# When the last node tiles choose their experts, and what fills the queues meanwhile

## The chip, the core and the metric

The kernel runs on one core of a Trainium2 chip. The core has five engines, each with its own in-order queue of instructions: PE (matrix products and transposes), DVE (element-wise work), ACT (activation functions, copies), POOL, which here issues the indirect transfers (gathers and scatters by a list of row numbers), and SP, which issues plain transfers. They wait for one another by semaphores. The metric is the device time of one execution in microseconds (us); a kernel is judged by the median over several runs.

## The reference

The program takes 6250 nodes with 256 features and 106250 edges (50000 random pairs in both directions, and a loop at each node). It applies four layers, each after a layer norm and with a residual: a two-step graph network (GIN), an attention over learned slices, a graph convolution (GCN), and a mixture of eight experts, of which each node uses two. Only the last two matter here:

```python
h = x @ W
msgs = h[src] * norm[:, None]
out = segment_sum(msgs, dst) + b
y = (out - running_mean) * rsqrt(running_var + BN_EPS) * gamma + beta
x = x + relu(y)

gate_logits = layernorm(x) @ Wg + bg + bias
topk_vals, topk_idx = top_k(gate_logits, 2)
topk_w = softmax(topk_vals)
h = relu(einsum('td,edh->teh', x_flat, W1) + b1)     # 256 -> 512, each expert
y = einsum('teh,ehd->ted', h, W2) + b2               # 512 -> 256
x = x + sum over the two chosen experts of topk_w * y
```

## The kernel before, in words

Nodes are worked on in 49 tiles of 128 rows (the last has 106). The end of the program joins the graph convolution and the experts in one stream; everything that the change touches is in it.

**Messages.** The edges, sorted by destination, are cut into 782 chunks of 128. For a chunk, POOL gathers the 128 source rows (`msg<-T`, by `gather`, L168) into a ring of 14 buffers, DVE builds a 0/1 matrix that says which row goes to which node (`hot`, L256), and PE multiplies the two in three products (L189, the table being kept in three bf16 pieces). A tile has 16 chunks, the last one 10. POOL issues up to 14 chunks ahead (`fetch_next` in `Sums.__call__`); `sums.n` counts the chunks issued and `others.n` is 782. When the chunks of half a tile are done, `add3` adds them into the tile's sum `s` (L1470, L1473).

**Slots.** While a tile's chunks are multiplied, `Sums.__call__` calls `between` seven times, evenly spread. Each call is a slot: `between_products(t, k)` with k from 0 to 6 puts other work there. Since PE, DVE, ACT and SP run their instructions in the order in which this code writes them, what is put in a slot stands in each of those queues between the tile's matmuls. `now[0]` counts slots, 7 to a tile.

**Choice.** `choice(i, ts, sent_at)` is a generator with seven steps for two tiles together: transpose the sums; multiply by the folded weights, add the residual (L1507 to L1512) and take the norm's statistics; finish the norm (L371 to L375); transpose; compute the gate's logits and the two best experts (L1528 to L1562); nothing; and places in the experts' lists (L1567 to L1577) with the shares (L1548 to L1551). One step is done per slot. It ends by putting the tiles into `to_send`.

**Send.** `send` scatters the tiles' rows into the DRAM table XD at their places, two scatters a tile on POOL (L1586). Then `advance` (L1610 to L1649), 24 small DVE instructions, works out which expert and first row each block of 128 rows will have. It is called where the count of issued messages reaches `sent_at`, or in the drain.

**Blocks.** A block is 128 rows of one expert: fetched by SP (`xd`, L1672, after two register loads, L1668 and L1669), transposed (L1693), multiplied by W1 (`ph`, L1699), transposed (L1705), activated on ACT (L1708), multiplied by W2 (`py`, L1713), given its bias on DVE (`yd`, L1714) and stored back in XD by SP (L1715). Two blocks overlap: a cycle of two pieces does the first half of one and the second half of the block before it. One piece goes into each slot (`next(block_pieces)`). SP keeps up to four blocks fetched ahead; yd has two buffers.

**Parts.** Tiles 0 to 39 are the first part, with its own table and 87 blocks; tiles 40 to 48 are the second, with 25. How many blocks of the second part may be started depends on the tiles sent: 1 after four tiles, 5 after six, 7 after seven, 9 after eight, all 25 after nine.

**Combine.** When all of a part's blocks are written into the program, its tiles enter `to_combine`. `combine` gathers a tile's two result rows per node (`g`, two gathers on POOL, L168, from a ring of eight buffers) and leaves an `end` to be run some slots later: two additions on DVE (L1752), and an output store on SP (L1494) once more than `keep` results are waiting.

**Drain.** After the last tile a loop goes on until nothing is left of choices, sends and blocks. Each step advances every choice, sends what is to be sent, does one piece of a block, and combines one tile. What is left of the combining follows in a second loop.

Before the change tiles 46 and 47 are chosen together during tile 48, tile 48 alone in the drain; pieces of blocks stop after the third slot of tile 48; nothing of the first part is combined before the drain.

Of the kernel before, what the change touches and what calls it, by code (L numbers as in the profile page):

```python
# [21 lines left out]
def gin_transolver_gcn_moe(ctx: ExitStack, tc: tile.TileContext, a: dict, out: bass.AP):  # L22
# [17 lines left out]
    NT = -(-N // P)  # L40
# [17 lines left out]
    def rows_of(t):  # L58
        return min(P, N - t * P)
# [11 lines left out]
    class Chunks:  # L71
# [5 lines left out]
        def start(self, k):  # L77

            return 0 if k <= 0 else self.n if k > 2 * NT - 2 else min(self.n, self.per * (2 * k + 1) // 4)

    all_edges, others = Chunks(E), Chunks(E - N)
# [85 lines left out]
    def gather(msg, table, ix):  # L167
        return nc.gpsimd.indirect_dma_start(out=msg, out_offset=None, in_=table,  # L168
                                            in_offset=bass.IndirectOffsetOnAxis(ap=ix, axis=0))
# [5 lines left out]
    def in_order(ins, gathers=True):  # L175
        for other in behind if gathers else behind[:1]:
            tc.add_manual_dep(ins.ins, other.name,
                              mybir.DependencyInfo(mybir.DependencyClass.NoSync,
                                                   mybir.DependencyReason.SCHED_ONLY),
                              reason="GpSimd's order")  # L180
        if gathers:
            behind.clear()
        behind.append(ins.ins)
# [274 lines left out]
    parts, Bs = [], []  # L458
    for upto, size in ((0.81, P), (1.0, P)):
        ts = [t for t in range(sum(map(len, parts)), NT) if (t + 0.5) / NT <= upto]  # L460
# [676 lines left out]
    if True:  # L1137
# [287 lines left out]
        sums = Sums(others, T3, None, 0, None, None, None)  # L1425
# [51 lines left out]
    sent = [[] for _ in parts]  # L1477
# [3 lines left out]
    TG, AHEAD = 2, 4  # L1481
# [3 lines left out]
    def load_ahead(t):  # L1485

        for u in range(t, min(t + 5, NT)):
            if u not in s3s:
                s3s[u] = w.tile([P, D], F32, name="s3", bufs=7)
                nc.sync.dma_start(s3s[u], S3[u])  # L1490

    def flush(keep):
        while len(outs) > keep:
            nc.sync.dma_start(*outs.pop(0))  # L1494
# [86 lines left out]
    def send(i, ts, xn):  # L1581

        for j, t in enumerate(ts):
            r = rows_of(t)
            for c in range(2):
                ins = nc.gpsimd.indirect_dma_start(  # L1586
                    out=XD[i], out_offset=bass.IndirectOffsetOnAxis(ap=place[:r, t, c:c + 1], axis=0),
                    in_=xn[:r, j, :], in_offset=None)
                in_order(ins, False)
                for other in sent[i] + taken[i] + stored[i]:  # L1590
                    tc.declare_no_dep(ins.ins, other, reason="no two rows go to one place")
                sent[i].append(ins.ins)
        final = ts[-1] == parts[i][-1]
        which = advance(i, final)
        rows = 2 * P * (ts[-1] + 1 - parts[i][0])
        n = n_blocks[i] if final else max(0, -((NE * (Bs[i] - 1) - rows) // Bs[i]))
        fresh.extend((i, which, no, len(sent[i])) for no in range(n_due[i], n))
        n_due[i] = n
# [57 lines left out]
    def load_experts(t):  # L1656

        for e in range(max(0, 2 * t), min(2 * t + 2, NE)):
            n = KD * HID
            nc.sync.dma_start(wx[:, e, :n].rearrange("p (k f) -> p k f", f=HID),  # L1660
                              a["L1_ffn_W1"][e].rearrange("(k p) f -> p k f", p=P))
            nc.sync.dma_start(wx[:, e, n:].rearrange("p (k f) -> p k f", f=D),
                              a["L1_ffn_W2"][e].rearrange("(k p) f -> p k f", p=P))
# [64 lines left out]
    due, fresh, ready, left = [], [], [], {i: n for i, n in enumerate(n_blocks)}  # L1728
    to_send, to_combine, ends = [], [], []
    n_due = [0 for _ in parts]  # L1730
    SLOTS = 7
    now = [0]

    def fetch_more():
        while len(ready) < AHEAD and due:
            b = due.pop(0)
            ready.append((b[0], fetched(*b)))

    def combine(when):

        i, t = to_combine.pop(0)
        r = rows_of(t)
        o = xr[:r, t, :]
        gs = []
        for c in range(2):
            g = w.tile([P, D], F32, name="g", bufs=8)
            in_order(gather(g[:r], XD[i], place[:r, t, c:c + 1]))
            gs.append(g[:r])

        def end():  # L1750
            for c in range(2):
                nc.vector.scalar_tensor_tensor(o, gs[c], share_of[:r, t, c:c + 1], o, op0=OP.mult, op1=OP.add)  # L1752
            flush(4)
            outs.append((out[t * P:t * P + r, :], o))
        ends.append((when, end))

# [8 lines left out]
    def blocks():  # L1765

        while True:
            pending[:] = block_of(*ready.pop(0)) if ready else None, pending[0]
            now_, last = pending
            for it in pending:  # L1770
                if it is not None:
                    next(it)
            if now_ is not None or last is not None:
                yield
            if now_ is not None:
                next(now_)
            if last is not None:
                next(last, None)
                pending[1] = None
            yield  # L1780

    block_pieces = blocks()

    def between_products(t, k):
        if k in (1, 4) and t + 1 < NT:
            of = 2 * t + 2 + k // 4
            if of <= 2 * NT - 2:
                sums.hot(of, start(of))
        if t >= EARLY // 2 and chains and next(chains[0], chains) is chains:
            chains.pop(0)  # L1790

        if t < NT - 1 or k < SLOTS // 2:
            next(block_pieces)
        run_ends()

    def run_ends():
        now[0] += 1
        while ends and ends[0][0] <= now[0]:
            ends.pop(0)[1]()

    def new_blocks():
        due.extend(fresh)
        fresh.clear()
        fetch_more()

    sums.beside = beside
    for i, ts_ in enumerate(parts):
        for q in range(0, len(ts_), TG):
            ts = ts_[q:q + TG]
            for t in ts:  # L1810
                load_ahead(t)
                load_experts(t - 1)
                s = s3s[t]

                nc.vector.scalar_tensor_tensor(s, xr[:, t, :], ln3[:, 0, t:t + 1], s, op0=OP.mult, op1=OP.add)
                k = iter(range(SLOTS))

                def between():
                    n = next(k, None)
                    if n is not None:  # L1820
                        between_products(t, n)

                now[0] = t * SLOTS
                sums(t, between, SLOTS)
                for n in k:
                    between_products(t, n)
                new_blocks()
            chains.append(choice(i, ts, min(others.n, start(2 * ts[-1] + 2) + 3 * others.per // 2)))
    while chains or to_send or due or ready or pending != [None, None]:
        for it in list(chains):  # L1830
            if next(it, chains) is chains:
                chains.remove(it)
        if to_send:
            send(*to_send.pop(0)[1:])
            new_blocks()
        next(block_pieces)
        if to_combine:
            combine(now[0] + 3)
        run_ends()
    while to_combine or ends:  # L1840
        if to_combine:
# [27 lines left out]
```

## Time and profile before

| what | value |
|---|---|
| median of 9 runs | 3551.62 us (3540.61 to 3554.55) |
| the profiled execution, its own time | 3544.95 us |
| its span, first to last instruction | 3542.5 us |
| PE busy in the span | 2803.3 us (79%) |
| POOL busy in the span | 2522.8 us (71%) |
| DVE busy in the span | 1647.7 us (47%) |
| ACT busy in the span | 866.6 us (24%) |
| mean granted PE clock | 0.919 |

A row of a timeline reads: start, duration (us), engine, line, operation, written tile, read tiles, shapes, number; in brackets the idle time of the engine before it and what ended that. A row of the chain that ended last has start, duration and the work or transfer. A row of the table of stretches has the stretch, its length, then for PE, weight loads, DVE, ACT and POOL the busy time and the number of instructions, then the granted PE clock (1.00 is full), the DMA engines' share and GB/s. "issue" means that the engine waited for nothing that the profile shows. Of the 190 us after tile 46 the table of stretches gives:

| stretch, us | PE busy | DVE busy | POOL busy | PE clock |
|---|---|---|---|---|
| 3300 to 3360 | 58.50 | 31.09 | 45.37 | 1.00 |
| 3360 to 3412 | 39.95 | 27.57 | 29.65 | 0.80 |
| 3412 to 3455 | 41.13 | 19.92 | 32.63 | 1.00 |
| 3455 to 3500 | 37.98 | 19.94 | 33.64 | 1.00 |
| 3500 to 3542.5 | 3.82 | 10.48 | 18.45 | 0.59 |

### The profile page before, as it was taken

The page shows a single profiled execution, that of the slowest core. Times are in us where ns is not written, and L with a number is a line of the kernel's source. Part 1 is how long each engine was busy: PE and PEld are TensorE (multiplying, and loading weights), DVE is VectorE, ACT ScalarE, POOL GpSimd, SP SyncE. Part 2 cuts the span into 40 slices and gives each one's busy share as a digit, 9 for nine tenths or more (in the row PEclk, how much of TensorE's full clock was granted, in tenths as well). Part 3 has the DMA queues.
Part 4 walks back from the last instruction along what each step waited for, and adds up shares of the span by engine and source line. Part 5 has one row for each costly group of instructions (what it writes and reads, how often), then busy time and mean ns, then how long its engine had stood idle before and what let it go on. Part 6 is the DMA issues. An engine that isn't in the chain of part 4 may idle for free.

```text
span 3542.5 us, 42536 instructions
## 1 busy us (share of the span) xinstructions
PE 2803.3 (79%) x12790; PEld 1701.6 (48%) x12854; DVE 1647.7 (47%) x4180; ACT 866.6 (24%) x1737; POOL 2522.8 (71%) x2618
## 2 busy tenths in 40 slices
PE   2667777777789699999999997956777777778984
PEld 1333344333346254454455444844555555556653
DVE  5465772232222254455554454754444444444453
ACT  4111111111113022212222122511222223323442
POOL 3777777777776677777777771377777777777765
PEclk7699999999999899999999998976888888889988
DMA  8667888888886899898889883785666666667656
GB/s 273 189 211 245 250 249 264 261 266 265 254 256 222 326 324 302 303 312 303 303 306 307 306 298 134 247 285 173 192 193 192 193 191 190 190 190 209 202 175 178
DMA packets 356553, 861.62 MB, mean 243 GB/s; under 512 B 60132, under 2 KB 158702, under 8 KB 356322
## 3 DMA queue, kind: packets, MB, share of 16 engines
q0 software_dynamic: 174688, 611.60, 55.9%
q1 hardware_dynamic: 175122, 237.62, 19.4%
q10 hardware_dynamic: 6512, 9.63, 0.8%
q8 instruction: 106, 1.74, 0.2%
q14 instruction: 125, 1.02, 0.1%
HBM read 691.35 MB, written 167.27 MB: 242 GB/s over the span
## 4 chain that ended last, share of the span: by engine, by line
PE 31%; DMA 22%; issue 5%; POOL 5%; DVE 2%; ACT 2%; POOLq 0%; ACTq 0%; DVEq 0%; SPq 0%
DMA msg<-T,srcT 14%; PE pa L189 8%; PE pa L283 5%; PE ph L1699 4%; PE py L1713 4%; POOL msg L168 3%; DMA XD<-xn,place 3%; DMA msg<-T2f,srcT 2%; DMA g<-XD,place 2%; PE ptok L1299 2%; PE pl L1274 2%; PE p L1250 1%; PE pt L417 1%; PE pn L1507 1%; PE po L1439 1%
## 5 line engine op out<-in xcount | busy, mean ns | idle before, releaser
L168 POOL DMA_INDIRECT msg<-T,srcT x2017 | 1944.7, 964 | 650.5 <-issue 265.2
L189 PE MATMUL pa<-msg,hot 128*128 128x256 bf16 (+2 forms) x5988 | 1127.9, 314 | 482.3 <-DMA msg<-T,srcT 462.4
L189 PEld LDWEIGHTS <-hot 128*128 128x128 bf16 x6177 | 622.2, 102 | 1148.2 <-issue 840.8
L256 DVE SCALAR_TENSOR_TENSOR hot<-dstT,node 128x1024 bf16<-128x1024 f32 (+2 forms) x255 | 310.4, 1218 | 30.4 <-PE pa L189 17.8
L168 POOL DMA_INDIRECT msg<-T2f,srcT x256 | 243.4, 951 | 78.0 <-issue 37.5
L283 PE MATMUL pa<-msg,hotf 128*128 128x512 f32 x512 | 244.6, 599 | 10.3 <-DMA msg<-T2f,srcT 9.8
L672 DVE TENSOR_TENSOR dinv<-dinv,pa 128x1 f32<-128x1 f32 x145 | 22.2, 153 | 453.7 <-PE pa L189 417.0
L1699 PE MATMUL ph<-wx,xdT 128*128 x448 | 214.1, 600 | 8.1 <-DVE yd L1714 4.7
L1713 PE MATMUL py<-wx,hT 128*128 x896 | 213.6, 381 | 0.7 <-ACT hT L1708 0.7
L1024 PE MATMUL p<-h1T,W1b 128*128 128x512 f32 (+2 forms) x480 | 206.8, 529 | 0.1
L1033 PE MATMUL p<-W2a,h2T 128*128 128x512 f32 x392 | 205.6, 613 | 0.0
L1713 PEld LDWEIGHTS py<-wx,hT 128*128 128x128 f32 x896 | 168.7, 190 | 65.0 <-issue 41.2
L301 DVE SCALAR_TENSOR_TENSOR s<-s,own,pa 128x512 f32<-128x512 f32 x97 | 71.9, 741 | 183.2 <-PE pa L189 115.1
L1708 ACT ACTIVATE hT<-pt,wb 128x128 f32<-128x128 f32 x448 | 127.7, 368 | 44.6 <-PE pt L1705 42.4
L283 PEld LDWEIGHTS pa<-msg,hotf 128*128 128x128 f32 x512 | 90.9, 190 | 94.0 <-issue 53.7
L168 POOL DMA_INDIRECT wx<-T,srcT x42 | 44.9, 1070 | 126.1 <-DVE ln L391 104.0
L1714 DVE TENSOR_TENSOR yd<-py,wb 128x256 f32<-128x256 f32 x112 | 47.2, 422 | 180.6 <-PE py L1713 179.0
L1586 POOL DMA_INDIRECT XD<-xn,place x98 | 97.7, 997 | 43.4 <-issue 29.2
L168 POOL DMA_INDIRECT msg<-T1f,srcT x80 | 86.5, 1081 | 56.4 <-DVE b1b L164 32.3
L1473 DVE TENSOR_TENSOR s<-s,pa 64x256 f32<-64x256 f32 x96 | 40.2, 419 | 185.4 <-PE pa L189 183.9
L168 POOL DMA_INDIRECT g<-XD,place x98 | 96.3, 982 | 39.4 <-issue 14.9
L1701 ACT ACTIVATE h<-ph 128x512 f32<-128x512 f32 x112 | 66.9, 597 | 213.1 <-PE ph L1699 213.1
(404 smaller groups left out, 3786.8 us busy)
## 6 DMA issues: line engine op xcount, KB each, us to landing
XD<-zeros SPq DMA_DIRECT2D x204, 256.0 KB
msg<-T,srcT POOLq DMA_INDIRECT x2017, 4.2
T<-tp SPq DMA_DIRECT2D x49, 384.0 KB
wb<-WB SPq DMA_DIRECT2D x112, 130.0 KB
xd<-XD SPq DMA_DIRECT2D x112, 128.0 KB
XD<-yd SPq DMA_DIRECT2D x112, 128.0 KB
T2f<-tf SPq DMA_DIRECT2D x49, 256.0 KB
s<-T2f SPq DMA_DIRECT2D x23, 512.0 KB
```

Of the source, the lines that this page charges most:

```text
L168: return nc.gpsimd.indirect_dma_start(out=msg, out_offset=None, in_=table, in_offset=bass.IndirectOffsetOnAxis(ap=ix, axis=0))
L189: ins = nc.tensor.matmul(pa[:, :n], hot, msg[:, s * F:s * F + n], start=(start and s == 2), stop=(stop and s == 1))
L256: nc.vector.scalar_tensor_tensor(hot[:, :n, :], self.edges.dst[:, c0:c0 + n, None].to_broadcast([P, n, P]), float(k * HALF), node2[:, k % ...
L283: self.last = nc.tensor.matmul(pa[:, :n], hot, msg[:, :n], start=ends[0], stop=ends[1])
L301: return nc.vector.scalar_tensor_tensor(at, at, times[rows], pa[rows, :F], op0=OP.mult, op1=OP.add)
L1024: nc.tensor.matmul(p[:, :T], W1b[:, k, m * P:(m + 1) * P], h1T[:, k, :T], start=(k == 0), stop=(k == KH - 1))
L1033: nc.tensor.matmul(p, h2T[:, k, j * P:(j + 1) * P], W2a[:, k, :], start=(k == 0), stop=(k == KH - 1))
L1274: nc.tensor.matmul(p, xnT[:, k, j * P:(j + 1) * P], Weff[:, k, :], start=(k == 0), stop=(k == KD - 1))
L1586: ins = nc.gpsimd.indirect_dma_start(out=XD[i], out_offset=bass.IndirectOffsetOnAxis(ap=place[:r, t, c:c + 1], axis=0), in_=xn[:r, j, :], ...
L1699: nc.tensor.matmul(p[:, :HID], xdT[:, k, :], W1[:, k, :], start=(k == 0), stop=(k == KD - 1))
L1708: nc.scalar.activation(hT[:, m, :], pt[:, m * P:(m + 1) * P], AF.Relu, bias=b1[:, m:m + 1])
L1713: nc.tensor.matmul(p[:, :D], hT[:, m, :], W2[:, m, :], start=(m == 0), stop=(m == KH - 1))
```

## The change

Four edits. In the last part, pairs are formed for the first six tiles only, so that tiles 46, 47 and 48 are each chosen by themselves; the choice of 46 runs in the slots of tile 47, that of 47 in the slots of tile 48. Pieces of blocks go into all seven slots of the last tile. A new function `behind_last` does, in a slot, what the drain does in a step: send what is to be sent, and combine a tile; it is called in every slot in which all 782 message chunks have been issued, and in the drain. Until all rows of the last part have been scattered it combines in odd slots only. And the output stores wait behind one further result, not four, once the last block is written.

```diff
         def end():
             for c in range(2):
                 nc.vector.scalar_tensor_tensor(o, gs[c], share_of[:r, t, c:c + 1], o, op0=OP.mult, op1=OP.add)
-            flush(4)
+            flush(4 if left[len(parts) - 1] else 1)
             outs.append((out[t * P:t * P + r, :], o))
...
-        if t < NT - 1 or k < SLOTS // 2:
-            next(block_pieces)
+        next(block_pieces)
+        if sums.n == others.n:
+            behind_last()
         run_ends()
+
+    def behind_last():
+
+        if to_send:
+            send(*to_send.pop(0)[1:])
+            new_blocks()
+        if to_combine and (len(sent[-1]) == 2 * len(parts[-1]) or now[0] % 2):
+            combine(now[0] + 3)
...
     for i, ts_ in enumerate(parts):
-        for q in range(0, len(ts_), TG):
-            ts = ts_[q:q + TG]
+        n_pairs = (len(ts_) - 2) // TG if i == len(parts) - 1 else len(ts_)
+        for ts in [ts_[q:q + TG] for q in range(0, len(ts_), TG)][:n_pairs] + [[t] for t in ts_[n_pairs * TG:]]:
...
         for it in list(chains):
             if next(it, chains) is chains:
                 chains.remove(it)
-        if to_send:
-            send(*to_send.pop(0)[1:])
-            new_blocks()
+        behind_last()
         next(block_pieces)
-        if to_combine:
-            combine(now[0] + 3)
         run_ends()
```

## The prediction

> **What bounds the kernel now.** I read the page first (span, section 2), then the chain of work that ended last from 3405 us on, then the timelines of POOL, DVE and PE around the last tiles, then the table of stretches. The change reaches only what comes after tile 46, the last 190 of 3542.5 us, so only that is worked out. The chain, backwards:
>
> ```profile
> 3485.06 3.77 DMA g<-XD,place
> 3488.94 3.22 DMA g<-XD,place
> 3492.82 3.85 DMA g<-XD,place
> 3498.05 3.46 DMA g<-XD,place
> 3502.45 1.88 DMA XD<-yd
> 3504.45 1.72 DMA XD<-yd
> 3506.29 1.73 DMA XD<-yd
> ```
>
> The last blocks' rows (XD<-yd) are stored right behind gathers of the first part, because one DVE queue serves both: each pair of L1752 additions waits for its gather, and the yd additions queue behind it. POOL's own timeline shows the ends of that queue and two holes:
>
> ```profile
> 3373.38 0.95 POOL L168 DMA_INDIRECT msg<-T,srcT  x1 [0.30 <-issue]
> 3388.02 1.02 POOL L1586 DMA_INDIRECT XD<-xn,place  x1 [13.69 <-issue]
> ...
> 3408.91 1.60 POOL L1586 DMA_INDIRECT XD<-xn,place  x1 [0.43 <-ACT h L1701]
> 3410.81 1.57 POOL L1586 DMA_INDIRECT XD<-xn,place  x1 [0.30 <-issue]
> ```
>
> ```profile
> 3498.05 0.95 POOL L168 DMA_INDIRECT g<-XD,place  x1 [0.30 <-DVE xr L1752]
> 3508.80 0.94 POOL L168 DMA_INDIRECT g<-XD,place  x1 [9.80 <-DMA XD<-yd]
> ```
>
> So the end is: the last scatter (tile 48's, done 3412.4), 68 gathers of the first part without a gap until 3499.0, that is (3499.0 - 3412.4)/68 = 1.27 us each, the last yd and its store, and 18 gathers from 3508.80 on. Two gather pairs belong to each block, 5.1 us of POOL against 4.46 us of PE (py to py in the quiet stretch 3405 to 3425), so PE is throttled, not throttling. What sets the last scatter is tile 48: its sum is added at 3387.60 and its choice then takes 20.8 us. Before it, the DVE timeline of tile 48:
>
> ```profile
> 3376.04 0.17 DVE L372 RECIPROCAL ln_sd<-ln_sd 128x2 f32<-128x2 f32 x1 [0.99 <-ACT ln_sd L371]
> 3376.24 0.16 DVE L373 SCALAR_TENSOR_TENSOR ln_sd<-ln_mv,ln_sd 128x2 f32<-128x2 f32 x1
> 3381.79 0.17 DVE L1530 TENSOR_TENSOR lg<-pg,gb 128x16 f32<-128x16 f32 x1 [5.39 <-PE pg L1528]
> ...
> 3387.60 0.48 DVE L1470 SCALAR_TENSOR_TENSOR s<-pa,ln,s 128x256 f32<-128x256 f32 x1
> 3388.00 0.16 DVE L1615 SCALAR_TENSOR_TENSOR f<-head,head 128x8 f32<-128x8 f32 x1
> ```
>
> L1615 opens the block planning of a send (24 small instructions, 3388.00 to 3392.12); it stands *behind* tile 48's sum here.
>
> **The change part by part.** I took the order of instructions on each engine from the built program of the changed kernel, and durations from these rows.
>
> *Tile 46 alone, during tile 47.* Its choice and send now come inside tile 47's seventh slot, ahead of tile 47's own last addition (L1473). Before, that addition ended its first half at 3365.4, right after its last matmul (3364.93). Now DVE first does the places and shares (3406.84 to 3408.61 in tile 48's choice: 1.8 us) and the planning (3408.53 to 3412.43: 3.9 us): 3364.9 + 0.2 + 5.7 + 0.4 = 3371.2, so tile 47 is whole 5.8 us later. PE then waits for it about 4 us. This is not on the path: its layer norm statistics are still done near 3375.3, and the next step waits longer.
>
> *Gathers of the first part, once all messages are issued.* POOL's order becomes: last message (its end 3374.33), 2 scatters of tile 46, 8 gathers, 2 scatters of 47, 6 gathers, 2 scatters of 48. Fourteen gathers, not twelve, stand ahead of the last scatter. The first two start at 3374.33 + 0.3 + 2 x 1.3 = 3377.2 and 3378.5. Their additions on DVE stand between tile 47's statistics and its reciprocal. From issue to addition took 3508.80 to 3511.48 (2.7 us) and 3510.05 to 3512.88 (2.8 us) with quiet queues, and 3498.05 to 3501.61 (3.6) with busy ones; here the messages have landed (DMA share 0.05 at 3376 to 3380, 0.00 after), so I take 2.8: second addition 3381.3 to 3381.8, tile 47's L373 done at 3382.2 against 3376.4: **+5.8 us**. Queued behind this wait are the choice of 47, the extra hot matrix of tile 48 (L256) and tile 48's sum. With the busy latency it is +6.6; it is zero if something else already holds DVE until 3382.
>
> [...]
>
> *Blocks through the last tile.* Two block cycles move into tile 48, between its matmuls. From L373 (3382.2): xn 0.6; transposes 0.5; ph 3.0 (3388.82 in the chain, the price after a PE pause; 1.72 at full clock) and py 1.73; two chunks 0.7 and pg 0.4: 3389.1. Choice on DVE after yd and two additions: 3389.55 + 2.7 = 3392.3. PE meanwhile: transposes 0.9, chunk 0.3, ph and py 3.45: 3393.8; yd and two additions until 3395.3, hot 0.3, last chunk and pp 0.8: 3396.4; places and shares 1.8; planning of 47 (now *ahead* of tile 48's sum) 3.9; sum 0.5: **3402.5** against 3388.08, +14.4. Of this 5.8 is the wait above; 8.6 is planning 3.9 plus 4.7, what 3.45 x 2 + 1.3 for the slow start + 2.8 for yd and additions leave after filling 6.3 of the 11.7 us that stood there (PE 2.38, DVE 5.39).
>
> [...]
>
> ```profile
> 3380.00:3384.00 4.00, 2.41 (x13) 1.86 (x11) 1.87 (x11) 0.96 (x1) 0.00 (x0) 0.50 0.00 2
> 3384.00:3388.00 4.00, 0.86 (x5) 0.58 (x5) 2.70 (x19) 0.21 (x1) 0.00 (x0) 0.50 0.00 0
> 3392.00:3396.00 4.00, 3.96 (x20) 3.01 (x19) 1.97 (x7) 1.74 (x6) 3.08 (x4) 1.00 0.37 111
> ```
>
> [...]
>
> *Choice of 48.* As before 20.8 us after its sum, less 1.1: only two additions, not four, precede its places (3405.01 to 3406.84). Last scatter: 14.4 - 1.1 = **+13.3**.
>
> *After it.* 66 gathers, not 68: 2 x 1.27 = **-2.5**. In the drain the gathers used to end 2.9 us of block work before the last yd; now only one yd follows: last addition (3502.09) to first gather of the second part (3508.80) was 6.7 us, now 0.4 for yd and 2.5 for the store (3506.29 to 3508.80) plus 0.1: **-3.7**. Cover for PE: 22 instead of 24 cycles follow tile 48's sum. From the last scatter, rows of the final lot arrive about 7 us later (fetch issued 3417.18, 4.8 us after 3412.4, plus 2.2), then 16 cycles x 4.46 and 6 to the last py: 84.4, against 66 x 1.27 + 3.1 = 87 for the gathers. The cover is 2.6 us thin. SP fetches three blocks (2.2 us each: 3364.37, 3366.69, 3368.91) before the next store, where one stood before; I charge **+0.5** (0 to 4). The 18 last gathers stay. The shorter queue of output stores costs and saves nothing: 14 of them follow the last yd store either way.
>
> Sum: 13.3 - 2.5 - 3.7 + 0.5 = +7.6, rounded to **+7.5 us**. The profiled execution took 3544.95 (span 3542.5 and 2.45 around it) and would take 3552.5. The median of nine, 3551.62, lies 6.7 above it, so I predict 3559.1, +0.21%. About 0.2% (7.1 us) is what a measurement can tell from no change.
>
> Bounds of the unknowns: clock after pauses -1.3 to +1.3 (one slow ph fewer or more), gather latency -0.5 to +0.8, scatters at 1.0 instead of 1.6 each -1.2 (as tile 44's) to 0, fetches -0.5 to +3.5: about +4 to +13 together, 3555.6 to 3564.6.
>
> **The rivals.** *Faster: the last scatter is not late.* If the pauses in tile 48 (POOL 13.69, PE 2.41, 2.38 and 2.49) really take up two blocks and the first gathers, only the gains of the end are left: -6.2, 3545.4. For it speak those pauses; against it that DVE's order puts gather waits and a planning ahead of tile 48's sum. It decides from a last scatter less than 6.2 us late, before 3415.1. Chance 0.18.
>
> *The wait for the first gathers is not paid* (DVE reaches them after they have landed): 7.5 - 5.8 = +1.7, 3553.3, no change to be seen. Against it: 6 us of slack between 3375.3 and 3381.3. Chance 0.16.
>
> *Blocks become the bound of the end:* SP's three fetches hold back a store, yd has two buffers, PE idles; 2 more fetches x 2.2 and the cover gone: +11.5, 3563. In the trace before, DVE waited 1.41 us once for such a store. Chance 0.14.
>
> That it doesn't do what it says holds for one part: the gathers gain only two places in POOL's order, since until the last part is sent they come in every second slot. That is in the sum.
>
> **How the numbers follow.** The forecast has 0.52; a third of it, 0.17, lies under 7.1 us. Slower: 0.35 + 0.14 + 0.01 = 0.50. Same: 0.17 + 0.14 = 0.31. Faster: 0.18 + 0.01 = 0.19. The range reaches from the faster rival, 3545, to 3566, the upper bound of the forecast with some of the block rival.
>
> **What would show it.** Right: DVE L1752 first appears in tile 48 before L372, idle there 5 to 7 us for DMA g; two blocks' py before tile 48's sum; last scatter near 3422; POOL idle twice around 10 us before it and for 6 us, not 9.8, after the first part's last gather. Wrong: a last scatter before 3415, or PE waiting on DMA xd in the drain for more than 5 us.

## The result, and the profile after

| | before | after |
|---|---|---|
| median, all runs of it beside the other | 3548.15 us (53 runs) | 3556.41 us (17 runs) |
| the profiled execution, its own time | 3544.95 us | 3550.61 us |
| its span | 3542.5 us | 3548.2 us |

The ratio is 1.0023, with a 95% interval of 1.0017 to 1.0029: the change costs 8.2 us of 3548 (6.0 to 10.3). The forecast was +7.5 us, 3559.1. The absolute figure lies 2.7 above the median because its base, the median of nine runs, lies 3.5 above that of all 53. The loss is measured, but the interval lies across the 0.2% that was named as the bound of what can be told apart. The experiments further down ran in three groups of four; in the first and third the kernel before itself took 4142.28 and 4181.19 us, 17 to 18% more than the 3541.68 of the second, for a reason not found, so the second group carries the argument.

The two profiled executions aren't in step: in the later one, the last message gather on POOL ends 3.7 us earlier (3370.66 against 3374.33 us). To compare the ends of the kernels, times below are offsets from this moment, called M.

| us after M | before | after | difference | forecast |
|---|---|---|---|---|
| tile 47's sum complete (L1473 ends) | -8.49 | -2.59 | +5.9 | +5.8 |
| tile 47's norm finished (L373 ends) | 2.07 | 7.86 | +5.8 | +5.8 |
| tile 48's first half added (L1470 ends) | 13.75 | 27.94 | +14.2 | +14.4 |
| last scatter starts | 34.58 | 48.68 | +14.1 | +13.3 |
| last gather of the first part ends | 124.67 | 138.13 | +13.5 | +11.3 |
| first gather of the second part starts | 134.47 | 143.68 | +9.2 | +7.6 |
| end of the span | 168.17 | 177.54 | +9.4 | +7.6 |

POOL's own timeline of the changed kernel, the rows that answer to those of before: the last message, the tiles' scatters, the first gathers, and the two ends of the gather queue.

```profile
3369.71 0.95 POOL L168 DMA_INDIRECT msg<-T,srcT  x1 [0.30 <-issue]
3370.96 1.00 POOL L1586 DMA_INDIRECT XD<-xn,place  x1 [0.30 <-issue]
3373.56 0.98 POOL L168 DMA_INDIRECT g<-XD,place  x1 [0.30 <-issue]
...
3394.68 1.00 POOL L1586 DMA_INDIRECT XD<-xn,place  x1 [11.36 <-ACT hT L1708]
...
3419.34 1.59 POOL L1586 DMA_INDIRECT XD<-xn,place  x1 [14.80 <-issue]
...
3514.34 0.95 POOL L168 DMA_INDIRECT g<-XD,place  x1 [5.55 <-DMA XD<-yd]
```

There are two long holes ahead of scatters, not one, and the last hole is 5.55 us, not 9.80. Between the last scatter and the last gather of the first part lie 66 gathers in 86.0 us.

The DVE timeline over tiles 47 and 48 shows what now stands ahead of tile 48's sum:

```profile
3363.09 0.16 DVE L1615 SCALAR_TENSOR_TENSOR f<-head,head 128x8 f32<-128x8 f32 x1
3367.20 0.87 DVE L1473 TENSOR_TENSOR s<-s,pa 64x256 f32<-64x256 f32 x2
3373.46 0.18 DVE L368 BATCH_NORM_AGGREGATE ln_mv<-ln_st 128x2 f32<-128x6 f32 x1
3376.34 0.48 DVE L1752 SCALAR_TENSOR_TENSOR xr<-g,share_of,xr 128x256 f32<-128x256 f32 x1 [2.70 <-DMA g<-XD,place]
3377.76 0.48 DVE L1752 SCALAR_TENSOR_TENSOR xr<-g,share_of,xr 128x256 f32<-128x256 f32 x1 [0.94 <-DMA g<-XD,place]
...
3378.36 0.16 DVE L373 SCALAR_TENSOR_TENSOR ln_sd<-ln_mv,ln_sd 128x1 f32<-128x1 f32 x1
...
3394.24 0.16 DVE L1615 SCALAR_TENSOR_TENSOR f<-head,head 128x8 f32<-128x8 f32 x1
3398.13 0.47 DVE L1470 SCALAR_TENSOR_TENSOR s<-pa,ln,s 128x256 f32<-128x256 f32 x1
...
3405.04 0.42 DVE L1714 TENSOR_TENSOR yd<-py,wb 128x256 f32<-128x256 f32 x1 [6.44 <-PE py L1713]
...
3418.20 0.17 DVE L1577 CAST place<-pl 128x2 int32<-128x2 f32 x1
3419.40 0.15 DVE L1549 TENSOR_SCALAR best<-best 128x1 f32<-128x1 f32 x1 [1.03 <-ACT best L1548]
```

A planning (it opens with L1615) runs ahead of tile 47's last half (L1473) and another ahead of tile 48's first half (L1470). The first two gathers are waited for between the statistics of tile 47 (L368) and its L373. The last three rows belong to the choice of tile 48: DVE waits 6.44 us for PE at the first `yd` behind the sum, and 1.03 us for ACT after `place`, the last thing that the scatter needs from DVE, is written.

PE's timeline of the same stretch, with the two pauses that follow from it:

```profile
3367.77 0.66 PE L417 MATMUL pt<-ident,s 128*128 128x128 f32 x2 [4.21 <-DVE s L1473]
...
3379.47 0.50 PE L417 MATMUL pt<-ident,xn 128*128 128x128 f32 x2 [3.82 <-ACT xdT L1695]
3379.76 3.56 PE L1699 MATMUL ph<-wx,xdT 128*128 x4
...
3398.76 0.66 PE L417 MATMUL pt<-ident,s 128*128 128x128 f32 x2 [4.58 <-DVE s L1470]
3399.21 3.62 PE L1699 MATMUL ph<-wx,xdT 128*128 x4
3402.62 2.38 PE L1713 MATMUL py<-wx,hT 128*128 x8
...
3406.62 1.98 PE L1699 MATMUL ph<-wx,xdT 128*128 x4
```

Four products `ph` take 3.56 and 3.62 us right after pauses of 3.82 and 4.58 us, and 1.98 us a little later. The table of stretches has the granted clock that goes with it (the column with 0.61 and 0.50):

```profile
3380.00:3384.00 4.00, 4.00 (x8) 1.87 (x8) 0.00 (x0) 1.32 (x4) 2.71 (x3) 0.61 0.34 98
3396.00:3400.00 4.00, 1.25 (x3) 0.79 (x4) 2.40 (x17) 0.38 (x1) 3.08 (x4) 0.50 0.31 102
```

The chain that ended last, in the place where before four gathers were followed by three stores of the last blocks in a row:

```profile
3505.35 3.66 DMA g<-XD,place
...
3509.51 0.43 DVE yd L1714
...
3509.95 1.73 DMA XD<-yd
...
3511.79 1.76 DMA XD<-yd
```

From 3446 us on, the chain runs mostly through gathers and their additions, until the last yds, which queue on DVE behind additions (from 3421 to 3446 us it runs through the last scatter's landing, a fetch and PE). Only one yd (3511.07) and its store are left after the last addition (3510.67): this is the shorter tail.

### The profile page after: what moved, and what is told of

It reads as the page before. It is cut to its first block, busy times and chain, and to the rows that moved or that the text cites. A ratio compares the mean times of both kernels' runs of the same rounds, so it can differ in the third digit from the quotient of the medians.

```text
span 3548.2 us, 42585 instructions
## 1 busy us (share of the span) xinstructions
PE 2813.5 (79%) x12792; PEld 1703.3 (48%) x12856; DVE 1656.1 (47%) x4228; ACT 869.2 (24%) x1743; POOL 2520.3 (71%) x2618
## 3 DMA queue, kind: packets, MB, share of 16 engines
q14 instruction: 127, 1.03, 0.1%
## 4 chain that ended last, share of the span: by engine, by line
PE 32%; DMA 22%; issue 5%; POOL 4%; DVE 3%; ACT 2%; POOLq 0%; ACTq 0%; DVEq 0%; SPq 0%
DMA msg<-T,srcT 14%; PE pa L189 7%; PE pa L283 4%; PE ph L1699 4%; PE py L1713 4%; POOL msg L168 3%; DMA XD<-xn,place 3%; PE ptok L1299 2%; PE pl L1274 2%; DMA msg<-T2f,srcT 2%; DMA g<-XD,place 2%; PE p L1250 1%; PE pt L417 1%; PE pn L1507 1%; PE po L1439 1%
## 5 line engine op out<-in xcount | busy, mean ns | idle before, releaser
L1473 DVE TENSOR_TENSOR s<-s,pa 64x256 f32<-64x256 f32 x96 | 40.2, 419 | 181.1 <-PE pa L189 179.5
```

## The experiments

The theory after the result: the loss is made ahead of tile 48's sum, on DVE's queue, by two things that can be moved: the additions that wait for the first gathers, and the planning of tile 47's send. The rival: it is made by the blocks themselves, those that went into the last tile or those of the drain with their fetches by SP, so that moving DVE work gives nothing. A second rival is the choice of single tiles.

Each run is compared with the kernel before in its own group. Differences in us are the ratio's part of that time: 0.1% of 3541.68 is 3.5 us. In the first and third group the intervals are about ±0.2% wide, and those runs are used for little.

### The second group: what stands ahead of tile 48's sum

**Additions later.** The eight gathers issued in slots are kept, but land in message buffers that are free by then, and their additions are done at the end of the drain.

```diff
+            if early:
+                g = sums.ring[(sums.at[others.n - 14 + 2 * len(held) + c] - len(sums.apart)) % 14].bitcast(F32)[:, :D]
+            else:
+                g = w.tile([P, D], F32, name="g", bufs=8)
...
-        ends.append((when, end))
+        if early:
+            held.append(end)
+        else:
+            ends.append((when, end))
...
-            behind_last()
+            behind_last(True)
...
+        elif held and not early and not to_combine:
+            held.pop(0)()
```

> The same kernel as e4 (the changed kernel with the slots' gathers landing in free message buffers and their additions at the end of the drain), once more. If the kernel before runs in about 3550 us here, my theory: tile 47's norm 4 to 6 us earlier than in the changed kernel, the last scatter 4 to 6 us earlier, +2 to +4 us against before. The rival, that PE or DVE is held at that place by something else anyway: no change from the changed kernel, +8 us.

Measured: 3549.19 us against 3541.68, ratio 1.0019 (1.0009 to 1.0028), +6.7 us (3.2 to 9.9): less gained than expected, and not told apart from the changed kernel's 1.0023.

**Planning of tile 47 later.** The send of tile 47, and with it the planning, goes to the first step of the drain, behind tile 48's sum:

```diff
-        if to_send:
+        if to_send and now[0] != NT * SLOTS - 1:
             send(*to_send.pop(0)[1:])
```

> The changed kernel, but tile 47 is sent in the first step of the drain, so that the planning (24 DVE instructions, 3.9 us) stands behind tile 48's sum, as the planning before it did. My theory: tile 48's sum and the last scatter 3.5 to 4 us earlier than in the changed kernel, +4 to +5 us against before. The rival, that the planning is hidden: no change from the changed kernel, +8 us.

Measured: 3545.82 us, 1.0009 (1.0000 to 1.0018), +3.2 us (0 to 6.4): about as expected.

**Both** edits together:

> Both edits of e5 and e6 on the changed kernel. My theory: the two gains add up, last scatter 8 to 10 us earlier than in the changed kernel, -2 to +1 us against before: the change without these two costs is about neutral. The rival, that they overlap, or that the drain is then bound by blocks: +3 us or more.

Measured: 3542.82 us, 1.0006 (0.9997 to 1.0015), +2.1 us (-1.1 to 5.3): 1 us above the range expected, no longer told apart from before, and better than the changed kernel's 1.0017 to 1.0029 (each against its own runs of before).

| us after M | before | after | additions later | planning later | both |
|---|---|---|---|---|---|
| L1473 of tile 47 ends | -8.49 | -2.59 | -1.60 | -2.88 | -2.02 |
| L373 of tile 47 ends | 2.07 | 7.86 | 6.25 | 7.83 | 5.95 |
| L1470 of tile 48 ends | 13.75 | 27.94 | 23.73 | 23.73 | 19.54 |
| last scatter starts | 34.58 | 48.68 | 44.64 | 42.04 | 37.84 |
| POOL idle before the second part's first gather | 9.80 | 5.55 | 7.73 | 6.57 | 8.72 |
| end of the span | 168.17 | 177.54 | 173.68 | 169.57 | 168.63 |

The theory holds and the first rival falls as the main cause: with the blocks left where the change puts them, moving DVE work alone takes 8.4 us off tile 48's sum (27.94 to 19.54) and 10.8 off the last scatter. The two gains at the sum, 4.2 each, add up, and the rest, +5.8 over before, stays; single choices and blocks were not parted in it.

The table also corrects a step. The wait for the first gathers is worth little at L373. Measured from the end of L1473, L373 ends 10.45 us later in the changed kernel and 10.71 with the planning moved, but 7.85 and 7.97 where no additions stand in the way: 2.6 us, not 5.8. (Before it was 10.56, for two tiles at once: one tile alone is done faster, and the gathers take that up.) The DVE timeline of the run with the additions later says what is late next there:

```profile
3370.25 0.87 DVE L1473 TENSOR_TENSOR s<-s,pa 64x256 f32<-64x256 f32 x2
...
3376.52 0.18 DVE L368 BATCH_NORM_AGGREGATE ln_mv<-ln_st 128x2 f32<-128x6 f32 x1
3378.61 0.16 DVE L372 RECIPROCAL ln_sd<-ln_sd 128x1 f32<-128x1 f32 x1 [1.91 <-ACT ln_sd L371]
```

Tile 46's planning, until 3370.22, is still ahead of L1473, so tile 47's sum, its statistics and a wait of 1.91 us for ACT's square root (0.99 before) come one after the other. The lateness of tile 47's sum now sets L373, where the wait for the gathers did.

As tile 47's sum came 1.0 us later in this run, only 1.6 of the 4.2 us show at L373. The other 2.6 come after it, and most of them on PE: with the additions gone PE pauses 1.92 us ahead of the transposes of `xn`, not 3.82, its four products `ph` take 1.88 us, not 3.56, and the `yd` behind them comes 1.7 us sooner after L373. The remaining 0.9 is a pair of additions (3390.95 in the changed kernel); the pair at 3385.43 gains nothing, as DVE then waits for PE.

The additions held back cost at the end of the drain: POOL is idle 7.73 us there, 2.2 more than after, and four held additions of 1.92 us (3508.23) stand right ahead of the last yd (3510.06). Shorter gathers in this profile (84.5 us against 86.0) and 0.5 us in the second part make up for it, so the trace ends 3.9 us earlier after M than the changed kernel's, +5.5 against before, while the ratio says +6.7 (3.2 to 9.9). How much of the 4 us is left in the time is not settled by these runs.

Moving the planning gains 6.6 us at the last scatter, not only 4.2. PE's timeline of the run with both edits shows the other 2.4 in its second place (the first is the place of the 1.92 and 1.88 above, which this run has too):

```profile
3379.58 0.44 PE L417 MATMUL pt<-ident,xn 128*128 128x128 f32 x2 [1.92 <-ACT xdT L1695]
3379.85 1.88 PE L1699 MATMUL ph<-wx,xdT 128*128 x4
...
3392.35 0.41 PE L417 MATMUL pt<-ident,s 128*128 128x128 f32 x2 [1.01 <-ACT hT L1708]
3392.60 1.88 PE L1699 MATMUL ph<-wx,xdT 128*128 x4
3394.32 1.89 PE L1713 MATMUL py<-wx,hT 128*128 x8
```

and here is the first of these places where only the planning is moved (in the second, the run has 1.01 and 1.88 too):

```profile
3387.32 0.69 PE L417 MATMUL pt<-ident,xn 128*128 128x128 f32 x2 [4.36 <-ACT xdT L1695]
3387.80 3.06 PE L1699 MATMUL ph<-wx,xdT 128*128 x4
```

Where PE pauses 1.01 or 1.92 us, the four products take 1.88; after pauses of 3.82 to 4.58 us they take 3.06 to 3.62. In the changed kernel the pause of 4.58 us before tile 48's transposes is the planning; it costs 3.62 + 2.38 - 1.88 - 1.89 = 2.2 us more behind it. The kernel before pays part of this too, though its pauses are shorter:

```profile
3377.85 1.11 PE L417 MATMUL pt<-ident,xn 128*128 128x128 f32 x4 [2.41 <-ACT xdT L1695]
...
3388.14 0.69 PE L417 MATMUL pt<-ident,s 128*128 128x128 f32 x2 [2.49 <-DVE s L1470]
3388.62 3.23 PE L1699 MATMUL ph<-wx,xdT 128*128 x4
3391.68 1.89 PE L1713 MATMUL py<-wx,hT 128*128 x8
```

In the kernel before the granted clock is 0.50 from 3380 to 3388 us, behind a pause of 2.41 us and through two more of 2.38 and 2.49, and the four products then take 3.23 us. What decides between 1.92 and 3.82 us is not shown here.

**Before, with early gathers.** The kernel before, unchanged in its choices, sends and blocks, with one thing of the change added: in odd slots after the last message a tile is gathered, into free message buffers, with the additions held back as in the run with the additions later.

```diff
         if t < NT - 1 or k < SLOTS // 2:
             next(block_pieces)
+        if sums.n == others.n and to_combine and now[0] % 2:
+            combine(0, True)
         run_ends()
```

> The kernel before with one thing from the change: eight gathers of the first part in the slots of the last tile, in the pause of 13.7 us of the gather queue, landing in free message buffers; their additions come at the end of the drain. Choices in pairs and blocks as before. My theory: the last scatter stays where it was, 60 instead of 68 gathers follow it, the gather queue is done 10 us earlier and the blocks (4.46 us each) set the end: 5 to 7 us faster than before. The rival, that the gathers were hidden beside the blocks: no change.

Measured: 3538.23 us against 3541.68, ratio 0.999 (0.9981 to 0.9999), -3.5 us (0.4 to 6.7 faster): faster than the kernel before, by less than expected. POOL's timeline of it, around the last scatter and at the end of the first part's gathers:

```profile
3372.32 0.95 POOL L168 DMA_INDIRECT msg<-XD,place  x1 [0.31 <-issue]
3381.55 1.02 POOL L1586 DMA_INDIRECT XD<-xn,place  x1 [2.04 <-issue]
...
3402.77 1.59 POOL L1586 DMA_INDIRECT XD<-xn,place  x1 [0.96 <-ACT h L1701]
...
3501.14 0.94 POOL L168 DMA_INDIRECT g<-XD,place  x1 [17.70 <-DMA XD<-yd]
```

The hole of 13.69 us ahead of the scatter is filled (2.04 is left). Sixty gathers follow the last scatter, not 68, and take 77.2 us instead of 86.6: 9.4 gained. But POOL then stands idle 17.70 us for the last yd, 7.9 more than before. Now the blocks set the end: from 3481 us on the chain that ended last runs through them, and their last `py` is only 1.2 us earlier when both are counted from tile 47's sum. So of the 9.4 us taken from the gather queue only 1.5 were left (9.4 - 7.9). In this profile the end lies 3.1 us earlier after M (165.09 against 168.17), but tile 47's sum, ahead of everything that the edit touches, is already 0.3 earlier there (M-8.83 against M-8.49). Counted from that sum the end comes 2.7 us sooner: 1.0 by the last scatter, 1.5 by the gathers less the longer hole, and 0.2 behind it. That stands beside the 3.5 of the ratio.

### The first and third group: one part undone at a time

Three single reversals, and a later version of the additions, ran in the first group; the three again, with one new kernel, in the third.

**Pairs back**, in the changed kernel, so that 46 and 47 are chosen together:

```diff
-        n_pairs = (len(ts_) - 2) // TG if i == len(parts) - 1 else len(ts_)
+        n_pairs = len(ts_)
```

> The changed kernel, but tiles 46 and 47 are chosen together as before; blocks through the last tile and gathers in the slots stay. My theory, that waits and work ahead of tile 48's sum make the last scatter late and that the last scatter then sets the end, expects about the changed kernel's time, +6 to +10 us against before: the gather wait, the planning ahead of tile 48's sum and the two block cycles are all still there. The rival, that choosing one by one is what costs (more small instructions, a planning more), expects +4 us or less.

> The same kernel as e1 (the changed kernel with tiles 46 and 47 chosen together), once more. My theory: the wait, the planning and the block cycles remain, and only five blocks of the last part are known until the pair is sent, so +6 to +12 us against before. The rival, that choosing one by one is what costs: +4 us or less.

Measured: 1.0008 (0.999 to 1.0027) and 1.0031 (1.0007 to 1.0054).

**Blocks stop** in the last tile, as before:

```diff
-        next(block_pieces)
+        if t < NT - 1 or k < SLOTS // 2:
+            next(block_pieces)
```

> The changed kernel, but pieces of blocks stop after the third slot of the last tile as before. My theory prices the two block cycles at 4.7 us of lateness of tile 48's sum and finds the drain bound by gathers, not blocks: last scatter 4 to 5 us earlier than in the changed kernel, time about +3.5 us against before. The rival, that blocks set the end, expects two more cycles in the drain to cost 4.5 to 9 us: +12 to +17 us against before.

> The same kernel as e2 (the changed kernel, pieces of blocks stop after the third slot of the last tile), once more. If the kernel before runs in about 3550 us here, my theory: tile 48's sum and the last scatter 4 to 5 us earlier than in the changed kernel, gathers still set the end, +3 to +4.5 us against before. The rival, that blocks set the end: two more cycles in the drain, +12 us or more.

Measured: 1.0009 (0.9989 to 1.003) and 1.0001 (0.9978 to 1.0024).

**No gathers in slots:**

```diff
-            behind_last()
+            behind_last(False)
...
-        if to_combine and (len(sent[-1]) == 2 * len(parts[-1]) or now[0] % 2):
+        if gathers and to_combine and (len(sent[-1]) == 2 * len(parts[-1]) or now[0] % 2):
```

> The changed kernel, but nothing is combined in the slots; the drain is as changed (every second step until all is sent). My theory: tile 48's sum 5 to 7 us earlier, but eight more gathers after the last scatter (74 instead of 66, 10.2 us), so 3 to 5 us slower than the changed kernel, +11 to +13 us against before. The rival, that the gathers after the last scatter are hidden beside the blocks, expects only the gain of the wait: +1 to +3 us against before.

> The same kernel as e3 (the changed kernel, nothing combined in the slots, 74 gathers after the last scatter), once more. In the late-additions kernel the wait turned out to be worth 4.2 us at tile 48's sum, so my theory: last scatter 4 us earlier than in the changed kernel, 10.2 us more of gathers after it, +13 to +16 us against before. The rival, that the gathers after the last scatter are hidden beside blocks: +3 to +5 us.

Measured: 0.9996 (0.9977 to 1.0015) and 1.0009 (0.9986 to 1.0031).

**Additions later**, the same kernel as in the second group:

> The changed kernel with the same order on the gather queue, but the eight gathers of the slots go into message buffers that are free by then, and their additions come at the end of the drain, so that nothing waits for them in tile 48. My theory: tile 47's norm 4 to 6 us earlier, tile 48's sum and the last scatter 4 to 6 us earlier, time +2 to +4 us against before. The rival, that PE or DVE is held at that place by something else anyway, expects no change from the changed kernel, +8 us.

Measured: 1.0004 (0.9985 to 1.0024).

**Both moves, and a gather pair in every step of the drain** (the diff is to the kernel with both):

```diff
-        if to_combine and (len(sent[-1]) == 2 * len(parts[-1]) or now[0] % 2):
+        if to_combine and (not early or now[0] % 2):
             combine(now[0] + 3, early)
```

> The kernel of e7 (additions late, planning behind tile 48's sum), with a tile combined in every step of the drain as in the kernel before, not in every second one until all is sent: 60 gathers instead of 66 after the last scatter. My theory: e7 was bound by gathers (its last one ended 8.7 us before the next part's first), so the end comes 5 to 8 us earlier than e7's: 4 to 8 us faster than before, and faster than e8 by 1 to 4. The rival, that blocks then set the end without delay: within 2 us of e7, no change against before.

Measured: 0.9997 (0.9972 to 1.0021). Only one of the eight intervals excludes 1, and each spans 8 to 10 us to either side: as times they settle little on a matter of 8 us. Their waits show that even their traces don't answer for the second group. POOL's waits, first in the run without gathers in slots:

```profile
POOL msg L168 <- PE pa L189: 359.0, 388, 5.8
...
POOL g L168 <- DVE xr L1752: 33.9, 18, 6.6
```

and in the changed kernel, as profiled for the result:

```profile
POOL msg L168 <- PE pa L189: 153.8, 505, 0.3
...
POOL g L168 <- DVE xr L1752: 7.6, 23, 0.9
```

(The numbers are the sum in us, how often, and the longest.) POOL waits for a free message buffer and a free `g` up to 5.8 and 6.6 us at a time there, and the mean granted clock is 0.842 to 0.854 instead of 0.92. The gathers after the last scatter take 109.2 us for 66 in the first run with pairs back (1.65 each) and 119.5 for 74 in the second without gathers in slots (1.61), where they took 1.27 to 1.30; a single issue still takes 0.95 us with 0.30 ahead of it, as in the kernel before. So the rate at which POOL can issue is not what limits the end there.

One reading is left, of the order among these kernels. The last scatter lies 51.9 and 52.5 us after M with the blocks stopped, 55.0 and 55.1 without gathers in slots, 58.0 with the additions later, 59.3 with both moves and more gathers, and 65.5 and 67.6 with pairs. Pairs are worst both times, and the only kernel with an interval above 1. That speaks for the single choices within the changed kernel, but the changed kernel itself wasn't run in these groups, so no price follows.

## Why the prediction was right, point by point

The direction, the size and the path were right: +7.5 us forecast, +8.2 measured, and the sum built from a late last scatter less a shorter end. Two of its terms missed, by 1.0 and 1.9 us, and two delays that run side by side were priced as one; the trace is 1.8 us above the forecast, and that the ratio is only 0.7 above it, within 6.0 to 10.3, proves nothing finer. The terms fared as follows.

- **Tile 46 alone, 5.8 us later for tile 47's sum, "not on the path".** The size is right (5.9, PE waiting 4.21 us for L1473 where about 4 was said). It is hidden behind the gathers in the changed kernel, but not by the slack that was forecast. The statistics end at M+2.98, when 3375.3 - 3374.33 = M+1.0 was worked out, and where nothing else stands ahead of it L372 waits 1.9 us for ACT. Without the additions L373 is still 4.2 us late.
- **The wait for the first gathers, +5.8.** The total at L373 is right (+5.8), because the landing was right: first gather issued 2.9 us after M, as forecast (3377.2 - 3374.33), and 2.8 us from issue to addition (3373.56 to 3376.34), as taken from the rows. The -0.5 for the gather latency among the bounds is shown by no run: from issue to addition the rows cited have 2.7 to 3.6 us before, and the first two gathers after took 2.8 and 2.9. But the term was counted as the gathers' alone, and only 2.6 of it are theirs: two delays run side by side, and the gathers are the later one by that much. So the rival "the wait is not paid" had a wrong price: it would leave about +5, not +1.7. Nor did DVE idle 5 to 7 us there, as named among the signs, but 2.70 + 0.94.
- **Blocks and planning ahead of tile 48's sum, +8.6.** L373 to sum grew from 11.68 to 20.08, 8.4 us. Planning: 4.2 by the experiment, or 3.9 between the two runs with the additions moved (17.48 - 13.59); 3.9 forecast. Blocks with yd and additions: 4.2 are left, 4.7 forecast, of which 2.3 go when the additions are moved (20.08 - 15.90 is the planning, 15.90 - 13.59 the additions with both edits); part of that is the clock, below. Two `py` stand ahead of the sum, at 3383.16 and 3388.68, as forecast.
- **Last scatter, +13.3; measured +14.1.** From tile 48's sum to the scatter 20.74 us passed, against 20.83 before: 0.1 gained, not 1.1. The two additions less are there (1.00 us at 3416.35 against 1.91 at 3405.01). But the first `yd` behind the sum comes 0.9 us later, because PE's `ph` and `py` ahead of it take 3.62 + 2.38 us where they took 3.23 + 1.89. The DVE row before:

```profile
3393.61 0.42 DVE L1714 TENSOR_TENSOR yd<-py,wb 128x256 f32<-128x256 f32 x1 [1.49 <-PE py L1713]
```

  It starts 5.53 us after the sum; in the changed kernel 3405.04 is 6.44 after it. So this step was mis-sized: it took PE to be as slow behind the sum as before, and PE was slower after the longer pause (4.58 us against 2.49). DVE's wait of 1.03 us for ACT (3419.40) has no part in it, as the scatter had started at 3419.34.
- **Two gathers fewer, -2.5; measured -0.6.** The gathers took 1.30 us each on average instead of 1.27 (66 x 0.03 = 2.0 us). 0.6 of this is one wait for DVE at 3439.00 (0.92 where 0.30 is usual); the other 1.4 are longer issues, 16 of 66 over 1.0 us where it was 9 of 68. This too was mis-sized; the wait belongs to the next point, the longer issues are unexplained.
- **Three fetches by SP, +0.5 (0 to 4).** They came as said, and did hold back a store. SP's timeline of the changed kernel:

```profile
3427.85 0.35 SPq L1672 DMA_DIRECT2D xd<-XD  x1
...
3432.50 0.33 SPq L1672 DMA_DIRECT2D xd<-XD  x1
...
3434.98 0.35 SPq L1715 DMA_DIRECT2D XD<-yd  x1
```

  What followed is in the rows of PE, DVE and POOL, one timeline each:

```profile
3430.16 0.66 PE L1693 MATMUL pt<-ident,xd 128*128 128x128 f32 x2 [5.26 <-DMA xd<-XD]
```

```profile
3437.91 0.42 DVE L1714 TENSOR_TENSOR yd<-py,wb 128x256 f32<-128x256 f32 x1 [7.63 <-DMA XD<-yd]
```

```profile
3439.00 1.07 POOL L168 DMA_INDIRECT g<-XD,place  x1 [0.92 <-DVE xr L1752]
```

  PE's wait of 5.26 us for `xd` is over the 5 us that the prediction named as a sign against itself. It was a poor sign: DVE's wait of 7.63 us for the store reached POOL as a gap of 0.92 us, 0.6 more than usual, because the ring of eight `g` buffers lies between. The block rival, +11.5, came into view and did not decide: the last `py` ended at M+135.96, the last gather at M+138.13, so the blocks were 2.2 us short of being the bound (2.6 forecast).
- **The shorter tail, -3.7; measured -4.25** (9.80 to 5.55).
- **PE after a pause.** Ahead of tile 48's sum the forecast charged 1.3 us for one slow start; the trace has 1.7 there (3.56 against 1.88). A second one has no term in the sum, only a place in the bounds (one slow `ph` more, +1.3). It came behind tile 48's sum: 0.9 us against before, whose own `ph` there was slow too, and 2.2 against a version that avoids the pause.

From M to the end this makes 14.1 - 0.6 - 4.25 + 0.2 (rounding and rows of the second part) = 9.4, against 7.6. The ratio says 8.2. Since M in single profiles varies by several us (3369.51 to 3378.53 over the six profiles that are not of the first and third group), a difference of 1 us between trace and ratio has no meaning.

The faster rival (the last scatter not late) is refuted: it came at 3419.34 in a profile that was 3.7 us ahead, past the 3415.1 named.

What stays open: the price of single choices against pairs, and of block cycles in the last tile taken alone, in runs like the second group's; tile 46's planning ahead of tile 47's last addition, which was not moved by itself; whether a gather pair in every step of the drain, on top of both moves, beats the kernel before with early gathers; what lowers the clock in pauses between 1.92 and 3.82 us; and the cause of the first and third group's times.

## What to carry to other kernels

Filling a pause on one queue is only free if nothing it brings along is queued ahead of the chain that made the pause: here the gathers filled POOL's holes, but their additions and a planning stood on DVE ahead of the sum that sets the last scatter, and the kernel before with the holes filled and the additions held back was the only version that came out faster than before. Look at the third queue too: while DVE stood in the wait, PE paused as well, and its next products took 3.56 us instead of 1.88. Price a wait against what else would be late at the same instruction, not against an empty queue: two delays that run side by side look like the sum of one, and removing it gives only the difference. And before shortening the queue that sets the end, look how far behind the next one is; here 9.4 us of gathers were worth 1.5, because the blocks came right behind.

## What the runs showed that was not expected

- In the first run without gathers in slots POOL waits 247.3 us in all for "remote" on its way to messages, a wait that the profiles before and after don't list, and in the profiled runs of the first and third group the mean granted clock is 0.842 to 0.854, not 0.92.
- The last tile's indirect transfers, of 106 rows, take longer on POOL than those of 128: 1.59 and 1.56 us against 1.00 for scatters (3419.34, 3421.23 and 3394.68 in the changed kernel), and 1.58 and 1.81 against 0.95 for the second part's last two gathers (3534.35, 3536.23 and 3533.10). They also take longer to land: in the chain that ended last, 6.43 us for the last scatter (3421.23) and 6.40 for the last gather (3536.23), where gathers of 128 rows of the second part took 2.87 to 3.09.
